# Four graph layers on one core: where one unit's division and normalization run (ScalarE or VectorE)

## The chip, the cores and the metric

The kernel runs on one core of a Trainium2 chip. The metric is the time of one execution on the device in microseconds; several executions give a median. The engines are named as the profile names them: PE is TensorE (PEld its weight loads), DVE is VectorE, ACT is ScalarE, POOL is GpSimd, SP is the queue that issues most of the DMAs.

## What is computed

The input x has 8 batches of 2048 nodes with 64 features; adj is a 2048 x 2048 matrix of edges that all batches share. Four layers follow each other, and each adds its result to x and normalizes every row over its 64 features. Cut to what matters here:

```python
# layers 0, 1, 2: attention over the edges, for each batch
s1, s2 = h @ a1, h @ a2                       # h is x times a weight matrix
e = leaky_relu(s1[:, :, None] + s2[:, None, :], 0.2)
att = softmax(where(adj > 0, e, -large), axis=-1)
h_prime = att @ h                             # then elu (layers 0, 1) or relu (layer 2)
x = layernorm(x + activation(h_prime))
# layer 3: softplus features, a softmax per feature over the edges
feat = softplus(x * c + b0)
attn = softmax(where(adj, feat * wa + ba, -large), axis=2)
x = layernorm(x + einsum(attn, feat))
```

The code counts layers from 0: "layer 1" in the code is the second layer, "layer 2" the third.

## The kernel before, in words

**Units and tiles.** A unit is one layer of one batch, written (layer, batch). The list `todo` (line 1243) orders the 24 units of the attention layers: (0,0) to (0,3), (1,0) to (1,3), (0,4) to (0,7), (1,4) to (1,7), then (2,0) to (2,7). A unit has 16 tiles, one for each block of 128 source nodes, and `attend` (line 902) computes one: a 128 x 2048 tile w of attention weights, and four matmuls that multiply it with the features and add to two PSUM tiles `acc`. In layers 0 and 1 VectorE makes w in one operation. In layer 2 a tile takes three engines in turn: GpSimd clamps a row (`clamp`, line 884, two tiles ahead), ScalarE takes two exponentials of 1024 columns into PSUM (`exponential`, line 893; two PSUM buffers), VectorE multiplies each with the edges. Four w buffers are there, so a clamp must wait until TensorE is through with the tile four places earlier.

**The order of the work.** Every engine takes its instructions in the order in which the program issues them (`InOrder`, line 68). The main loop issues the tiles; between two tiles it calls `bg.step()` once, which moves every generator in a list of background streams (`Streams`, line 1209) one step ahead. A generator that yields 2 sits out a step. So the number of yields in a stream decides between which tiles its later parts land. Streams that need a PSUM buffer of the pool `pm` (two buffers) wait their turn in `pm_slots`; `Banks.width()` says whether a stream may take both at once.

**The end of a unit** is such a stream: `finish` (line 949), begun right after the unit's last tile, so that it runs among the tiles of the unit behind it. ScalarE copies the sums to `oT`; TensorE multiplies them with a matrix (`p_o`, four products in PSUM, the 65th column of each half being the divisor); the division follows (lines 988 to 1006): a reciprocal `den` on VectorE, then, for layers 0 and 1, 16 ScalarE operations of 128 x 64, each with its own scale, and for layer 2 four VectorE operations of 128 x 256. Then the activation and the sum with x; `stats` (line 486) makes the row sums and `inv_std` the factor rs (a power on GpSimd) and the shift nm. The normalization follows (lines 1033 to 1045): 16 ScalarE operations of 128 x 64 with a yield after every fourth for layers 0 and 1, or two VectorE operations of 128 x 1024 for layer 2. A result that layer 1 or 2 goes on with is stored one column to the right, with a column of ones ahead of the features (`Rows`, line 158); its 64th feature lies in a column of its own for each block, and `settle` copies it there on GpSimd and writes the ones.

**Behind the end of (1,7)** the same stream goes on with `scores(2, 7)` (transposes `p_xT`, copies `xTv`, products `p_s`, the copy `s`), and then with `group(1)` (line 758), which makes the bounds of the clamps for the units (2,4) to (2,7): small VectorE operations on `lc`, `lim`, `sc`, `s2`, `tt`, `hi`, `lo`; 256 small matmuls `p_lse` in 8 pieces of 32, one piece in each step, and then `am`, `amT` and a DMA to the rows that unit (2,4) reads.

**Layer 3** is made of streams too: `l3_features` of a batch follows its unit of layer 2 (softplus `sp` and `f` on ScalarE with two loads of the function table, `vf`, and splitting into three bf16 parts `v`), and `l3_products` multiplies edges with a pair of batches once both are ready. `now` holds the layer of the unit whose tiles are being issued, and that unit's place in `todo`; after the last unit, now[0] is 3.

All of these operations are recorded through one helper, so the profile gives line 78 for all of them: groups are told apart by the names of their tiles. In these names layer and batch are left out, so `x<-o,st_x` stands for the normalization of every unit.

Of the kernel before, what the change touches and what calls it, by code (L numbers as in the profile page):

```python
# [14 lines left out]
ALU = mybir.AluOpType  # L15
# [33 lines left out]
def gnn4_kernel(ctx: ExitStack, tc: tile.TileContext, t, out):  # L49
# [3 lines left out]
    K = N // P  # L53
# [51 lines left out]
    class Banks:  # L105
# [4 lines left out]
        pool = None  # L110
# [28 lines left out]
    pe, dve, act, pool = (InOrder(e) for e in (nc.tensor, nc.vector, nc.scalar, nc.gpsimd))  # L139

    def psum(name):
        return pm.tile([P, 512], F32, tag="pm", name=name)

    def bc_f(v, n=K, f=F):
        return v[:, :, None].to_broadcast([P, n, f])

    def bc_k(v, n=K, f=F):
        return v[:, None, :].to_broadcast([P, n, f])
# [337 lines left out]
    def stats(y, n, name):  # L486

        st = small.tile([P, 2, n], F32, tag="st", name=f"st_{name}", bufs=4)
        yield from sq_slots.take()
        sq = tmp.tile([P, n, F], F32, tag="sq", name=f"sq_{name}")  # L490
        act.activation(sq, y, AF.Square)
        dve.tensor_reduce(st[:, 0], y, AX.X, ALU.add)
        yield 2 if now[0] < 2 else 1
        dve.tensor_reduce(st[:, 1], sq, AX.X, ALU.add)
        sq_slots.give()
        yield from inv_std(st, n, name)
        return st[:, 0], st[:, 1]
# [451 lines left out]
    def finish(u):  # L949
        layer, b = u.layer, u.b  # L950
        yield from oT_slots.take()
        oT = tmp.tile([P, 2, 512], F32, tag="oT", name=f"oT_{u.n}")
        for c in range(2):
            act.copy(oT[:, c], u.acc[c])
        if layer == 0:
            hb = early.tile([P, K, F], F32, tag="hb", name=f"hb_{u.n}", bufs=1)
            for sl, y in V[0, b].parts:
                pool.tensor_tensor(
                    hb[:, :, sl], y, bc_k(gamma[:, sl], K, y.shape[2]), ALU.mult
                )  # L960
        yield 1
        yield from o_slots.take()
        o = tmp.tile([P, K, F], F32, tag="o", name=f"o_{u.n}", bufs=2)
        o5 = o.rearrange("p (c h s) f -> p c s h f", c=2, h=2)
        done = 0
        while done < 4:
            width = Banks.width()
            ps = []
            yield from pm_slots.take(width)
            for i in range(done, min(done + width, 4)):  # L970
                c, s0 = i // 2, 2 * (i % 2)
                p = psum(f"p_o_{u.n}_{c}_{s0}")
                for s in range(2):
                    k = s0 + s
                    pe.matmul(
                        p[:, s * 2 * F1 : (s + 1) * 2 * F1],
                        lhsT=oT[:, c, k * P : (k + 1) * P],
                        rhs=RH[layer].rearrange("p h f -> p (h f)"),
                        start=True,
                        stop=True,  # L980
                    )
                ps.append((c, s0, p))
            done += width
            if done >= 4:
                oT_slots.give()
            yield 2 if width == 2 else 1
            for c, s0, p in ps:
                p4 = p[:, : 4 * F1].rearrange("p (s h f) -> p s h f", s=2, h=2)
                den = small.tile([P, 2, 2], F32, tag="den", name=f"den_{u.n}_{c}_{s0}")
                dve.reciprocal(den, p4[:, :, :, F])  # L990
                if layer == 2:
                    dve.tensor_tensor(
                        o5[:, c, s0 : s0 + 2],
                        p4[:, :, :, :F],
                        den[:, :, :, None].to_broadcast([P, 2, 2, F]),
                        ALU.mult,
                    )
                    continue
                for s in range(2):
                    for h in range(2):  # L1000
                        act.activation(
                            o5[:, c, s0 + s, h],
                            p4[:, s, h, :F],
                            AF.Copy,
                            scale=den[:, s, h : h + 1],
                        )
            pm_slots.give(width)
        if layer == 2:
            for sl, x in x_cur[b].parts:
                dve.scalar_tensor_tensor(o[:, :, sl], o[:, :, sl], 0.0, x, ALU.max, ALU.add)  # L1010
            yield 1
        else:
            yield 1
            if layer == 0:
                pool.tensor_tensor(o, o, hb, ALU.add)
                yield 2

            yield from e_slots.take()
            e = tmp.tile([P, K, F], F32, tag="e", name=f"eh_{u.n}")
            act.activation(e, o, AF.Relu, scale=-1.0)  # L1020
            act.activation(e, e, AF.Exp, scale=-1.0)
            yield 1
            for sl, x in x_cur[b].parts:
                pool.tensor_tensor(
                    e[:, :, sl], e[:, :, sl], x, ALU.add
                )
            act.activation(o, o, AF.Relu)
            yield 1
            pool.tensor_tensor(o, o, e, ALU.add)
            e_slots.give()  # L1030
            yield 2
        nm, rs = yield from stats(o, K, f"x_{u.n}")
        xn = Rows(x_cur[b].t, layer < 2)
        if layer == 2:
            dve.tensor_tensor(o, o, bc_f(rs), ALU.mult)
            dve.tensor_tensor(xn.v, o, bc_f(nm), ALU.add)
        else:
            yield 1
            for k in range(K):
                act.activation(  # L1040
                    xn.block(k), o[:, k], AF.Identity, scale=rs[:, k : k + 1], bias=nm[:, k : k + 1]
                )
                if k % 4 == 3:
                    yield 1
            xn.settle()
        o_slots.give()
        x_cur[b] = xn
        V[layer + 1, b] = xn
        if layer < 2:
            yield 1  # L1050
# [7 lines left out]
    now = [0, 0]  # L1058
# [227 lines left out]
    for n, (layer, b) in enumerate(todo):  # L1286
# [31 lines left out]
        for jb in range(K):  # L1318
            if n == 0:
                while masks < min(K, 9 + jb):  # L1320
                    mask(p_deg, masks)
                    masks += 1
                    if masks == K:
                        empties(p_deg)
            attend(u, jb, handover)
            if jb == K - 1:
                end = [lambda u=u: finish(u)]
                if layer < 2:
                    end += [2 if now[0] < 2 else 1, lambda layer=layer, b=b: scores(layer + 1, b)]
                else:  # L1330
                    end += [1, lambda b=b: l3_features(b)]
                if layer == 1 and b % NB == NB - 1:
                    end += [lambda b=b: group(b // NB)]
                bg.add(chain(*end), begun=True)
            elif not done and jb >= 10 and ready(*nxt):
                prepare(*nxt)
                done = True
            if done and nxt is not None and nxt[0] == 2 and jb >= K - 2:
                clamp(*nxt, jb - (K - 2))
            if layer == 0 and jb == 2 and 6 <= b + 4 < B:  # L1340
                load_x(b + 4)
            if n == 0 and jb == 3:
                bg.add(constants())
            if jb == (1 if n < 2 else 4) and n in begin:
                bg.add(features0(begin[n]))
            bg.step()
# [517 lines left out]
```

## Time and profile before

| | us |
|---|---|
| median of 4 runs | 1572.63 (1569.91 to 1576.92) |
| the profiled execution | 1577.95 |
| its span, first to last instruction | 1576.1 |
| PE busy in the span | 1325.7 (84%) |
| DVE busy | 1298.0 (82%) |
| POOL busy | 811.2 (51%) |
| ACT busy | 801.1 (51%) |
| mean granted TensorE clock | 0.944 |

VectorE's products of layer 2 begin at 778.85 us; the units (2,0) and (2,1) take the stretch up to 907 us. The busy shares are means over stages with different limits, so a number for one stage is read from the timeline of that stage. Times in a timeline are microseconds from the start of the span, then the length, engine, operation, tiles and shapes. A bracket at the end gives the idle time of the engine ahead of this instruction, and what ended it. An instruction's length holds the time in which it waits for the memory access it needs, so equal instructions of different length tell of such waits.

### The profile page before, as it was taken

The page shows a single profiled execution, that of the slowest core. Times are in us where ns is not written, and L with a number is a line of the kernel's source. Part 1 is how long each engine was busy: PE and PEld are TensorE (multiplying, and loading weights), DVE is VectorE, ACT ScalarE, POOL GpSimd, SP SyncE. Part 2 cuts the span into 40 slices and gives each one's busy share as a digit, 9 for nine tenths or more (in the row PEclk, how much of TensorE's full clock was granted, in tenths as well). Part 3 has the DMA queues.
Part 4 walks back from the last instruction along what each step waited for, and adds up shares of the span by engine and source line. Part 5 has one row for each costly group of instructions (what it writes and reads, how often), then busy time and mean ns, then how long its engine had stood idle before and what let it go on. Part 6 is the DMA issues. An engine that isn't in the chain of part 4 may idle for free.

```text
span 1576.1 us, 20954 instructions
## 1 busy us (share of the span) xinstructions
PE 1325.7 (84%) x8130; PEld 658.6 (42%) x8130; DVE 1298.0 (82%) x1364; ACT 801.1 (51%) x1635; POOL 811.2 (51%) x742
## 2 busy tenths in 40 slices
PE   3668888988899899998878585899977989789996
PEld 2313333333333333433222131456543646477885
DVE  4798989988999999999878878978887888777444
ACT  4315454546465434344488657575756575552110
POOL 1153353344233434232476577577879687864332
PEclk9989999999999999999999789899988999889998
DMA  8720000000000000000000000000101000000000
GB/s 307 223 42 2 1 2 1 1 2 2 1 1 2 0 1 2 1 29 28 0 1 27 27 2 27 1 27 8 35 7 34 1 7 7 8 8 15 14 13 18
DMA packets 42190, 36.86 MB, mean 23 GB/s; under 512 B 37509, under 2 KB 37813, under 8 KB 39906
## 3 DMA queue, kind: packets, MB, share of 16 engines
q1 hardware_dynamic: 41538, 34.26, 7.0%
q8 instruction: 66, 1.08, 0.3%
q10 hardware_dynamic: 544, 1.17, 0.2%
q14 instruction: 42, 0.34, 0.1%
HBM read 30.94 MB, written 4.45 MB: 22 GB/s over the span
## 4 chain that ended last, share of the span: by engine, by line
PE 24%; DVE 20%; ACT 9%; issue 5%; POOL 5%; POOLq 0%; DVEq 0%; ACTq 0%
PE p_l L78 16%; DVE w L78 11%; PE acc L78 6%; ACT e L78 4%; DVE o L78 2%; DVE st_x L78 2%; ACT sp L78 1%; POOL w L78 1%; POOL vf L78 1%; DVE vf L78 1%; ACT x L78 1%; ACT v L78 1%; DVE fs L78 1%; POOL e L78 1%; PE p_o L78 1%
## 5 line engine op out<-in xcount | busy, mean ns | idle before, releaser
L78 DVE SCALAR_TENSOR_TENSOR w<-r,se,edge 128x2048 f32<-128x2048 f32 (+1 forms) x270 | 555.4, 2102 | 22.6 <-PE r L78 19.7
L78 PE MATMUL acc<-w,pv 128*64 128x512 f32 x2048 | 504.6, 624 | 74.2 <-DVE w L78 69.0
L78 PEld LDWEIGHTS <-edge 128*128 128x128 fp8e4 x3842 | 322.5, 99 | 126.8 <-issue 65.4
L78 ACT ACTIVATE e<-w,s_g 128x1024 f32<-128x1024 f32 x256 | 277.7, 1113 | 172.0 <-DVE w L78 127.7
L78 PE MATMUL acc<-w,x 128*64 128x512 f32 x1024 | 284.8, 673 | 89.1 <-DVE w L78 84.0
L78 PE MATMUL p_l<-v,edge 128*128 128x256 bf16 x3072 | 354.1, 276 | 0.6 <-ACT nd L78 0.6
L78 DVE TENSOR_TENSOR w<-e,edge 128x1024 f32<-128x1024 f32 x256 | 299.8, 1212 | 50.5 <-ACT e L78 48.7
L78 POOL TENSOR_SCALAR w<-row,hi_g,lo_g 128x2048 f32<-128x2048 f32 x128 | 275.1, 2154 | 42.9 <-PE acc L78 39.9
L78 PEld LDWEIGHTS acc<-w,pv 128*64 128x64 f32 x2048 | 132.2, 140 | 340.8 <-issue 183.3
L78 PEld LDWEIGHTS acc<-w,x 128*64 128x64 f32 x1024 | 64.5, 147 | 239.1 <-DVE w L78 170.6
L78 ACT ACTIVATE nd<-p_l,empty 128x256 f32<-128x256 f32 x64 | 29.9, 469 | 133.2 <-PE p_l L78 133.2
L78 ACT ACTIVATE x<-o,st_x 128x64 f32<-128x64 f32 x256 | 90.3, 443 | 4.2 <-DVE st_x L78 4.2
L78 ACT COPY oT<-acc 128x512 f32<-128x512 f32 x48 | 25.7, 586 | 126.8 <-PE acc L78 126.8
L78 ACT ACTIVATE o<-p_o,den 128x64 f32<-128x64 f32 x256 | 55.8, 325 | 49.9 <-DVE den L78 49.8
L78 POOL TENSOR_TENSOR st_h<-isw_h,mhalf 128x16 f32<-128x16 f32 x8 | 23.6, 2951 | 110.3 <-DVE isw_h L78 85.4
L78 PE MATMUL p_o<-rh,oT 128*128 128x130 f32 x384 | 60.4, 295 | 20.4 <-DVE st L78 13.2
L78 POOL TENSOR_TENSOR st_x<-isw_x,mhalf 128x16 f32<-128x16 f32 x24 | 71.1, 2962 | 2.0
L78 PEld LDWEIGHTS p_o<-rh,oT 128*128 128x128 f32 x384 | 49.6, 197 | 52.2 <-issue 32.9
L78 DVE TENSOR_REDUCE st<-sq 128x4 f32<-128x256 f32 x32 | 13.2, 414 | 65.3 <-ACT sq L78 65.3
L78 POOL TENSOR_SCALAR isw_x<-isw_x 128x16 f32<-128x16 f32 x24 | 6.3, 262 | 113.7 <-DVE isw_x L78 113.7
L78 POOL CAST rT<-rT 16x128 bf16<-16x128 f32 x45 | 15.0, 333 | 95.0 <-ACT rT L78 91.9
L78 POOL TENSOR_SCALAR isw<-isw 128x4 f32<-128x4 f32 x32 | 7.4, 231 | 104.3 <-DVE isw L78 99.7
(236 smaller groups left out, 1516.9 us busy)
## 6 DMA issues: line engine op xcount, KB each, us to landing
raw<-in_adjT_dram SPq DMA_DIRECT2D x8, 1024.0 KB
raw<-in_adjT_dram SPq DMA_DIRECT2D x16, 512.0 KB
row<-rows_d_g SPq DMA_DIRECT2D x8, 1024.0 KB
x<-in_x_dram SPq DMA_DIRECT2D x8, 512.0 KB
out_dram<-o SPq DMA_DIRECT2D x64, 64.0 KB
row<-row_d ACTq DMA_DIRECT2D x1, 1024.0 KB
row_d<-rT SPq DMA_DIRECT2D x15, 12.0 KB
row<-row_d SPq DMA_DIRECT2D x15, 12.0 KB
```

The lines of the kernel that those rows point to most:

```text
L78: ins = f(*args, **kwargs)
```

## The change

The condition that chooses VectorE for the division and the normalization is no longer the unit's own layer, but the layer whose tiles are being issued at that moment. Units of layer 2 always end at a time when that is 2 or 3, so nothing changes for them. Of the other 16 units, only (1,7) comes to these lines among tiles of layer 2. For it, the division is made by four VectorE products of 128 x 256, and the normalization by a product of 128 x 1024 and a sum in two parts, of 1008 columns and of 16, which write the shifted layout at once; GpSimd writes the ones. The five yields between the ScalarE operations aren't there in that branch.

```diff
@@ in finish
                 dve.reciprocal(den, p4[:, :, :, F])
-                if layer == 2:
+                if now[0] > 1:
                     dve.tensor_tensor(
                         o5[:, c, s0 : s0 + 2],
                         p4[:, :, :, :F],
@@ in finish
         nm, rs = yield from stats(o, K, f"x_{u.n}")
         xn = Rows(x_cur[b].t, layer < 2)
-        if layer == 2:
+        if now[0] > 1:
             dve.tensor_tensor(o, o, bc_f(rs), ALU.mult)
-            dve.tensor_tensor(xn.v, o, bc_f(nm), ALU.add)
+            for sl, y in xn.parts:
+                dve.tensor_tensor(y, o[:, :, sl], bc_f(nm, K, y.shape[2]), ALU.add)
+            if layer < 2:
+                pool.memset(xn.v[:, :, 0:1], 1.0)
         else:
             yield 1
             for k in range(K):
```

## Prediction

> **What bounds the kernel now.** Read first the page's costliest groups for the third layer: each tile takes two exponentials on ScalarE and two products on VectorE, and each waits for the other.
>
> ```profile
> L78 ACT ACTIVATE e<-w,s_g 128x1024 f32<-128x1024 f32 x256 | 277.7, 1113 | 172.0 <-DVE w L78 127.7
> ...
> L78 DVE TENSOR_TENSOR w<-e,edge 128x1024 f32<-128x1024 f32 x256 | 299.8, 1212 | 50.5 <-ACT e L78 48.7
> ```
>
> Two products need 2.4 us, two exponentials 2.2 us, and there are only two PSUM buffers between them. A tile left alone lasts 2.45 us (two exponentials start at 847.52, the next two at 849.99). Whatever stands between them on either engine is then paid, unless the other engine fills the same gap. Next, VectorE's timeline: unit (1,7) ends among the tiles of unit (2,0).
>
> ```profile
> 795.31 2.35 DVE L78 TENSOR_TENSOR w<-e,edge 128x1024 f32<-128x1024 f32 x2 [2.79 <-ACT e L78]
> ...
> 801.52 2.36 DVE L78 TENSOR_TENSOR w<-e,edge 128x1024 f32<-128x1024 f32 x2 [1.39 <-ACT e L78]
> ...
> 825.62 2.36 DVE L78 TENSOR_TENSOR w<-e,edge 128x1024 f32<-128x1024 f32 x2 [1.16 <-ACT e L78]
> ...
> 868.27 0.34 DVE L78 TENSOR_REDUCE lc_g<-s 128x4 f32<-128x64 f32 x2 [3.00 <-ACT s L78]
> ...
> 914.53 2.35 DVE L78 TENSOR_TENSOR w<-e,edge 128x1024 f32<-128x1024 f32 x2 [7.67 <-ACT e L78]
> ...
> 944.81 0.78 DVE L78 SCALAR_TENSOR_TENSOR st_x<-st_x 128x16 f32<-128x16 f32 x1
> 945.52 1.21 DVE L78 TENSOR_TENSOR o<-o,st_x 128x1024 f32<-128x1024 f32 x1
> 946.76 2.96 DVE L78 TENSOR_TENSOR x<-o,st_x 128x1024 f32<-128x1024 f32 x1
> ```
>
> In brackets stands how long VectorE had nothing to do. ScalarE's timeline names the cause of the first two, and of the 7.67 us:
>
> ```profile
> 792.57 1.71 ACT L78 ACTIVATE o<-p_o,den 128x64 f32<-128x64 f32 x8
> ...
> 798.75 1.73 ACT L78 ACTIVATE o<-p_o,den 128x64 f32<-128x64 f32 x8
> ...
> 829.07 1.42 ACT L78 ACTIVATE x<-o,st_x 128x64 f32<-128x64 f32 x4
> ...
> 910.46 1.07 ACT L78 COPY oT<-acc 128x512 f32<-128x512 f32 x2 [4.92 <-PE acc L78]
> ```
>
> The copy of unit (2,1)'s sums waits for TensorE, which the table of windows (its columns: length, then busy time and count of PE, PEld, DVE, ACT, POOL, then the granted clock) shows fully busy at half clock, and then at full:
>
> ```profile
> 900.00:910.00 10.00, 10.00 (x88) 3.43 (x84) 6.75 (x7) 4.68 (x5) 4.88 (x2) 0.50 0.00 0
> 910.00:920.00 10.00, 8.77 (x130) 4.83 (x130) 5.41 (x8) 9.23 (x10) 6.59 (x3) 1.00 0.01 2
> ```
>
> **The order of instructions** of both programs differs from tile 2 of unit (2,0) to tile 8 of unit (2,2) only; SP's queue is the same, DMA for DMA. One unit, (1,7), changes: 32 ScalarE operations and one GpSimd copy go, seven VectorE operations come. And because its end yields five times fewer, all that follows it moves up: the scores of (2,7), the bounds of the second group, the 8 pieces of 32 small matmuls (p_lse). The end of unit (2,0) and the features of its fourth layer move back, since they share PSUM buffers.
>
> **Part 1, the division.** In place of 8 operations, VectorE gets two products of 0.42 us that add 0.35 each to its queue (845.12 to 845.67 is a reciprocal with its product, 0.55; the reciprocal alone steps 0.2). First pair: VectorE stands idle 0.89 us before the product at 790.17, which hides them. ScalarE's exponentials start at 792.57 instead of 794.15: -1.6. Second pair: the distance of the next products falls from 3.74 to 2.45, that of the ones before grows from 2.47 to 3.36: -0.4. Sum **-2.0 us**. The second pair of matmuls p_o, which waited 3.27 us for ScalarE to free PSUM, comes earlier as well; nobody waits for it.
>
> **Part 2, the normalization on VectorE.** The trace has its twin: at 944.81 in unit (2,1) the same shift, product and sum stand beside GpSimd's clamps and end at 949.72, 4.9 us in all. The last column (16 elements, about 0.15) comes on top; 0.78 of it is there already, and 1.16 us of idle time before the product at 825.62 cover a part: 4.9 + 0.15 - 0.78 - 1.16 = **+3.1 us**. Queued behind it are the products of tile 13, and ScalarE and TensorE behind those; no other cover is left, as ScalarE has no long work there. Bounds: the fastest rows (1.21 + 1.30 + 0.16 - 1.16) give +1.5; the slowest of each form (1.76 for o, 2.96 for x, 3.37 for o<-o,x) give 8.1 - 1.2 = +6.9. I take the twin: five of the eight such sums took 2.96, three 1.30 to 1.36. GpSimd's clamps, five in a row from 822.39, lose some 2.4 us; they are two tiles ahead.
>
> The Trainium skill (SBUF — State Buffer, "Who interferes with whom") speaks against this part: a VectorE instruction with two SBUF inputs and a GpSimd instruction that reads SBUF exclude each other for a whole instruction. Were all three to wait for a clamp of 2.04 us each, this part would come to some +6; the rows show the first product at 1.21 or 1.22 in seven of eight cases, so one wait.
>
> **Part 3, the normalization off ScalarE.** Four insertions of 1.42 us go. A lone one costs 1.0 (exponentials at 826.94 and 830.40 are 3.46 apart, against 2.47). Tile 15: 3.03 becomes 2.45, -0.6. The next two distances, 3.55 + 4.37, fall to 6.1: the copy of the sums still waits for TensorE, 4.0 us after tile 15's product starts. That is -1.8. The fourth gives way to the move of two copies xTv (1.14 together) to that very place: -0.2. Sum **-2.6 us**. GpSimd loses a copy of 0.21 and gets its memset early: nothing, it had been idle 4.64 us.
>
> **Part 4, the new order in unit (2,1),** from its product at 839.44 to the 7.67 us. VectorE does the same instructions in another order, so I compare its stalls. Before: 1.05 (an x insertion, up to 842.85), 3.00 (lc_g), 3.2 (st_x 1.64 and x 2.96, beyond 0.17 and 1.21), 3.35 (tt_g 1.99 and 1.55 beyond 0.25 and 0.22, and an idle 0.28), 1.98 (idle before 881.01, softplus on ScalarE), 0.59 (f), 7.67: 20.8 us. After:
> - xTv: 0.7. It keeps PSUM from p_o for 2 us; TensorE catches up within two tiles.
> - lc_g, now behind tile 4: it waits for ScalarE's copy s behind two exponentials, 3.8 us after a product of 2.3 starts: 1.5.
> - st_x and x: 3.2 again.
> - the s_g block: te stands behind two exponentials (0.9); GpSimd has few free buffers there (1.0): 1.9.
> - softplus lies beside that block: 0. But f has only one product ahead of it, and ScalarE needs 1.28 + 1.06 + 1.22 first: 2.4.
> - the clamp for unit (2,2)'s first tile stands behind two GpSimd products of 2.36 that wait for f: 1.2.
> - the copy oT: from the start P of tile 14's product TensorE needs, at half clock, 1.3 + 3.68 + 1.01 + 0.69 + 3.68 + 0.44 = 10.8, then 1.07 for the copy and 1.04 for the exponential that now stands next, P + 12.9; VectorE is through at P + 8.3: 4.6. At full clock (1.94, 0.96, 0.35, 1.94, 0.41) the same sum is 0.8.
>
> Together 15.5: **-5.3 us**, or -9.1 at full clock. I take half clock, since 890 to 910 show it on the same operations, with gaps like those to come.
>
> The skill (TensorE: Matmul & The Clock Gate, "What's actually happening") says that a busy window of about 3.4 us gives full clock. By that, oT would not be late and the whole sum would be -8.5; here TensorE was busy for 10 us and stayed at 0.50, so the measurement decides.
>
> **Part 5, unit (2,2).** The block am_g now stands ahead of the end of unit (2,1), where GpSimd goes from clamps to v<-vf of 4.08 us. Before, it waited 1.1 (1.34) and 1.75 (1.99). If its second product meets the long one: +2.1. Lower bound -0.2 (no change but tile spacing), upper +6.6: three products and o<-o,x behind 2.04 + 4.08 + 2.04 + 2.04 = 10.2 against 3.6. I take **+2.1**: the long operation stands next in the queue.
>
> **Sum:** -2.0 + 3.1 - 2.6 - 5.3 + 2.1 = -4.7 us. The profiled execution took 1577.95 (its span 1576.1 and 1.85 around it) and would take 1573.2. The runs shown have a median of 1572.63, 5.3 below it; I set the same gain against that: **1567.9 us**. Behind unit (2,2) the order is unchanged and every engine is late or early together, so I expect the gain to last.
>
> **Rivals.**
> 1. Full clock: the new gaps let TensorE reach 1.00 before tile 14. 1572.6 - 8.5 = 1564.1. For it: 878 to 880, where it recovered within 4 us of busy time. Against: 890 to 910.
> 2. The stall only moves: TensorE's eight p_lse pieces are the same work, and what lc_g and oT save comes back at f and at the clamps, with part 5 at nothing. Parts 1 to 3 alone give -1.5: 1571.1. For it: 2.4 and 1.2 us above are new waits.
> 3. Slower: VectorE and GpSimd wait for each other at every place. Part 2 at +6.9, part 5 at +6.6, and 2.0 more for vf behind a clamp: -2.0 - 2.6 - 5.3 + 6.9 + 6.6 + 2.0 = +5.6, 1578.2. It decides once those waits exceed parts 1, 3 and 4, 9.9 us together. For it: 2.96 in five rows of eight. Against: GpSimd is often out of buffers (39.9 us idle behind acc).
> 4. More units than one change: the order of instructions excludes it.
>
> **Chances.** Forecast 0.38, full clock 0.19, moved stall 0.27, slower 0.16. The forecast lies at the edge of 0.3% (4.7 us, about what a measurement can tell), so half of its chance is below: faster 0.42, same 0.42, slower 0.16. Leaving out the slower case's upper part and the best bounds (part 2 at +1.5 with full clock and part 5 at -0.2, -12.4): 1561 to 1576.
>
> **What would show it.** Right: exponentials two by two without gap at tiles 4 to 6 of unit (2,0); x<-o,st_x of unit (1,7) near 3 us; lc_g's idle near 1.5; the stall before unit (2,2)'s second tile near 4.6 at a clock of 0.50. Wrong: that stall at 7 or more, or am_g's products at 4 us each. From tile 9 of unit (2,2) on, both traces should run at a constant distance; a drift there would break the sum.

## The result, and the profile after

| | median, us | runs |
|---|---|---|
| before | 1573.02 (1567.8 to 1578.55) | 55 |
| after | 1576.62 (1572.43 to 1581.13) | 34 |
| ratio | 1.0023 [1.0015, 1.003] | |
| forecast | 1567.9 (1561 to 1576) | |

The change makes the kernel slower by 0.23%, 3.6 us: the other sign than the forecast's -4.7, and 0.6 us above its range. The profiled execution of after took 1575.12, its span 1573.3. Against the profiled execution of before (1577.95) that would be a gain of 2.8. That two profiles and some 90 runs disagree in sign is part of what has to be explained.

The page of after, its costliest groups of the third layer (busy time, mean ns of one, idle time before them):

```profile
L78 ACT ACTIVATE e<-w,s_g 128x1024 f32<-128x1024 f32 x256 | 277.9, 1114 | 183.7 <-DVE w L78 144.2
...
L78 DVE TENSOR_TENSOR w<-e,edge 128x1024 f32<-128x1024 f32 x256 | 299.7, 1212 | 32.7 <-ACT e L78 30.6
```

VectorE's idle time ahead of its products fell from 50.5 us to 32.7. ScalarE's, ahead of its exponentials, rose from 172.0 to 183.7. So VectorE waits 17.8 us less ahead of its products, yet the span is only 2.8 shorter: VectorE's busy time grew, from 1298.0 us to 1311.2. VectorE's timeline of after, from the normalization of (1,7) on, shows where:

```profile
821.82 1.21 DVE L78 TENSOR_TENSOR o<-o,st_x 128x1024 f32<-128x1024 f32 x1
823.07 3.03 DVE L78 TENSOR_TENSOR x<-o,st_x 128x1008 f32<-128x1008 f32 x2
...
851.11 0.34 DVE L78 TENSOR_REDUCE lc_g<-s 128x4 f32<-128x64 f32 x2 [1.30 <-ACT s L78]
...
871.12 0.57 DVE L78 TENSOR_TENSOR sc_g<-lim_g 128x4 f32<-128x4 f32 x1
...
872.11 1.61 DVE L78 TENSOR_TENSOR beyond<-beyond,far_g 128x1 f32<-128x1 f32 x1
...
873.93 3.85 DVE L78 TENSOR_SCALAR sc_g<-sc_g 128x4 f32<-128x4 f32 x2
...
879.23 1.23 DVE L78 TENSOR_TENSOR x<-o,st_x 128x1024 f32<-128x1024 f32 x1
```

The normalization took what part 2 said (near 3), and lc_g's idle time is near 1.5. The tiny sc_g block, which the prediction did not list at all, is not cheap: its two multiplications of four columns took 3.85 us. In before they took:

```profile
884.41 0.34 DVE L78 TENSOR_SCALAR sc_g<-sc_g 128x4 f32<-128x4 f32 x2
```

What stands beside them in after is on GpSimd's timeline:

```profile
869.64 8.12 POOL L78 TENSOR_SCALAR w<-row,hi_g,lo_g 128x2048 f32<-128x2048 f32 x4
...
916.95 4.06 POOL L78 TENSOR_SCALAR w<-row,hi_g,lo_g 128x2048 f32<-128x2048 f32 x2
920.98 4.05 POOL L78 TENSOR_TENSOR v<-vf,v 128x2048 bf16<-128x2048 f32 x1
925.02 4.13 POOL L78 TENSOR_SCALAR w<-row,hi_g,lo_g 128x2048 f32<-128x2048 f32 x2
```

Four clamps of 2.04 in a row end at 871.68, 873.71, 875.73 and 877.76. Of VectorE's small operations the first sum of sc_g ends at 871.69, `beyond` at 873.72, and the two multiplications at 875.76 and 877.78: each ends with a clamp. Ten operations that had needed 1.67 us from first to last need 7.05. The same in unit (2,2), VectorE in after and then in before:

```profile
919.22 1.87 DVE L78 TENSOR_TENSOR am_g<-am_g,half_ldeg 128x64 f32<-128x64 f32 x1
921.12 3.99 DVE L78 TENSOR_TENSOR am_g<-am_g,sc_g 128x64 f32<-128x64 f32 x1
925.14 1.96 DVE L78 TENSOR_SCALAR am_g<-am_g 128x64 f32<-128x64 f32 x1
927.02 0.21 DVE L78 SCALAR_TENSOR_TENSOR tt_g<-s,sc_g 128x64 f32<-128x64 f32 x1
927.26 1.96 DVE L78 TENSOR_TENSOR am_g<-am_g,tt_g 128x64 f32<-128x64 f32 x1
```

```profile
931.37 1.34 DVE L78 TENSOR_TENSOR am_g<-am_g,half_ldeg 128x64 f32<-128x64 f32 x1
932.74 1.99 DVE L78 TENSOR_TENSOR am_g<-am_g,sc_g 128x64 f32<-128x64 f32 x1
934.77 0.20 DVE L78 TENSOR_SCALAR am_g<-am_g 128x64 f32<-128x64 f32 x1
```

The second product waits out the long v<-vf (it ends at 925.11, GpSimd's at 925.03), as part 5 said. The multiplication and the last operation, am_g<-am_g,tt_g, then wait for one more clamp each: 10.3 us for a block that took 4.28. In before the block meets only the end of a row of clamps:

```profile
925.58 9.08 POOL L78 TENSOR_SCALAR w<-row,hi_g,lo_g 128x2048 f32<-128x2048 f32 x4
```

The last two of the four end at 932.63 and 934.66. Its two products end with them (932.71 and 934.73); the three operations behind, from 934.77 on, find GpSimd idle and take 0.20 to 0.22 each.

**The same stretch by stages.** Distances between starts of VectorE's products, in us; (0) to (2) are the units (2,0) to (2,2). The column "in place" is the experiment of that name below.

| from, to | before | after | in place | what lies there |
|---|---|---|---|---|
| (0) tile 3, tile 13 | 35.5 | 36.5 | 36.5 | division, normalization |
| (0) tile 13, (1) tile 1 | 13.8 | 12.4 | 12.4 | insertions on ScalarE before |
| (1) tile 1, (2) tile 1 | 75.1 | 69.1 | 72.2 | scores, sc_g, s_g, features, oT |
| (2) tile 1, tile 9 | 35.1 | 40.2 | 35.1 | am_g, end of (2,1) |
| sum | 159.5 | 158.1 | 156.2 | |

After repeats well (158.1, 158.2, 158.1 in three executions). Before doesn't: six profiled executions gave 159.5, 156.6, 156.9, 156.9, 159.3 and 156.6. Of the 2.8 us by which the profile of after is shorter than that of before, 1.4 lie in this stretch; 0.6 lie ahead of it (layer 2's first product starts at 778.22 instead of 778.85) and 0.8 behind it, where both programs do the same in the same order.

### The profile page after: what moved, and what is told of

It reads as the page before. It is cut to its first block, busy times and chain, and to the rows that moved or that the text cites. A ratio compares the mean times of both kernels' runs of the same rounds, so it can differ in the third digit from the quotient of the medians.

```text
span 1573.3 us, 20925 instructions
## 1 busy us (share of the span) xinstructions
PE 1322.3 (84%) x8130; PEld 656.9 (42%) x8130; DVE 1311.2 (83%) x1371; ACT 792.7 (50%) x1603; POOL 811.3 (52%) x741
## 4 chain that ended last, share of the span: by engine, by line
PE 23%; DVE 20%; ACT 8%; POOL 4%; issue 3%; POOLq 0%; ACTq 0%; DVEq 0%
PE p_l L78 16%; DVE w L78 10%; PE acc L78 6%; ACT e L78 4%; DVE o L78 2%; DVE st_x L78 1%; ACT sp L78 1%; POOL vf L78 1%; DVE vf L78 1%; POOL w L78 1%; ACT v L78 1%; ACT x L78 1%; POOL e L78 1%; DVE x L78 1%; DVE nd L78 1%
## 5 line engine op out<-in xcount | busy, mean ns | idle before, releaser
L78 ACT ACTIVATE e<-w,s_g 128x1024 f32<-128x1024 f32 x256 | 277.9, 1114 | 183.7 <-DVE w L78 144.2
L78 DVE TENSOR_TENSOR w<-e,edge 128x1024 f32<-128x1024 f32 x256 | 299.7, 1212 | 32.7 <-ACT e L78 30.6
L78 ACT ACTIVATE x<-o,st_x 128x64 f32<-128x64 f32 x240 | 84.6, 444 | 3.2 <-DVE st_x L78 3.2
L78 ACT ACTIVATE o<-p_o,den 128x64 f32<-128x64 f32 x240 | 52.3, 325 | 51.3 <-DVE den L78 51.3
```

What stands on the lines that cost most here:

```text
L78: ins = f(*args, **kwargs)
```

## Experiments

The theory formed from these lines: **the order costs, not the engine.** The VectorE operations of parts 1 to 3 give what was forecast (-1.5), and what moves up with the five yields meets GpSimd's clamps, in the blocks sc_g and am_g. First rival: the VectorE operations themselves cost more than was seen, and the order gives part 4's gain. Second rival: these waits only fill time that VectorE would have waited anyway, so their end would bring nothing. Third: the runs of before are favoured by the way the two are timed. Where an expectation gives a letter, it stands for one such theory.

### The engine without the order, and the order without the engine

"In place" is after with the yields put back, so that every instruction stands where it stood in before:

```diff
             if layer < 2:
                 pool.memset(xn.v[:, :, 0:1], 1.0)
+                yield 5
```

> The division and the normalization of unit (1,7) on VectorE as in the change, but the five yields are put back behind them, so that every other instruction of all engines stands where it stood before. Theory A (the new order is what costs: it sets the small VectorE blocks sc_g and am_g beside GpSimd's clamps, and the profiled execution of before was a long one): parts 1 to 3 of the prediction alone, 1.5 us below before. Theory B (the VectorE operations themselves cost, in their place): the whole 3.6 us above before. Theory C (both small, the rest is a difference in TensorE's clock): within 1 us of before.

Measured: 1571.74 against 1572.88 for before, ratio 0.9994 [0.9974, 1.0013]. "Order alone" is before with ScalarE's operations and after's order:

```diff
-            yield 1
+            late_unit = now[0] > 1
+            if not late_unit:
+                yield 1
...
-                if k % 4 == 3:
+                if k % 4 == 3 and not late_unit:
                     yield 1
```

> Division and normalization of unit (1,7) stay on ScalarE, in 16 operations each, but its five yields are left out, so that everything behind it is ordered as in the change (the 16 normalization operations stand in one row on ScalarE). Theory A: 3.6 + 1.5 = 5 us above before, with sc_g's block near 7 us instead of 1.7 and am_g's near 10 instead of 4. Theory B: within 1 us of before. The 16 operations in one row cost ScalarE 5.7 us at one place, as much as in four places, so this adds 1 or 2 us under either.

Measured: 1580.42, ratio 1.0053 [1.0032, 1.0074], the slowest of all kernels here. Two things are in it. ScalarE has the 16 operations in a row, and VectorE's product waits for them; and the two blocks are as long as in after, sc_g 7.07 and am_g 10.32. ScalarE, then VectorE, in order alone:

```profile
826.19 5.39 ACT L78 ACTIVATE x<-o,st_x 128x64 f32<-128x64 f32 x16
```

```profile
832.62 2.35 DVE L78 TENSOR_TENSOR w<-e,edge 128x1024 f32<-128x1024 f32 x2 [4.83 <-ACT e L78]
...
925.42 3.99 DVE L78 TENSOR_TENSOR am_g<-am_g,sc_g 128x64 f32<-128x64 f32 x1
929.44 1.96 DVE L78 TENSOR_SCALAR am_g<-am_g 128x64 f32<-128x64 f32 x1
```

The first costs 3.6 (17.4 instead of 13.8 in its stage); it is of this experiment alone and no part of after. What follows: the order makes both kernels that have it slower, and after without it isn't slower than before. The first rival falls.

> The changed kernel once more, for a second trace. Theory A: sc_g's block again 4 to 7 us against 1.7, am_g's 8 to 10 against 4.2, the stretch from tile 3 of unit (2,0) to tile 9 of unit (2,2) again near 158 us. Theory C: these blocks vary by several us between traces, with the clock. In time 3.6 us above before, by either.

After once more, on the same chip: 1576.43, ratio 1.0022 [1.0006, 1.0038], stretch 158.2. Since the intervals of in place and of this one overlap by a little (1.0013 and 1.0006), the two kernels are told apart by their stages: the table puts the whole difference behind tile 1 of (2,1), where nothing but the order differs. It is 2.0 us there (-3.1 and +5.1); the medians are 4.7 apart.

### The halves of the change alone

"Division alone" has only the first condition of the diff in before, "norm alone" only the second, with the yields put back as above:

```diff
-                if layer == 2:
+                if now[0] > 1:
                     dve.tensor_tensor(
                         o5[:, c, s0 : s0 + 2],
```

> Only the division of unit (1,7) on VectorE; normalization, yields and order as before. Part 1 of the prediction: the stretch from tile 3 to tile 13 of unit (2,0) 2.0 us shorter (35.5 before), the time 2 us below before or, by theory E, 1 us above it. If the trace shows less than 1 us there, part 1 was mis-sized.

Measured: 1572.68 against 1572.27, 0.9989 [0.9969, 1.001]. Timing can't show 2 us, the trace can: from tile 3 to tile 13 of (2,0) 33.52 instead of 35.45. That is -1.9 (part 1: -2.0).

> Only the normalization of unit (1,7) on VectorE, with its five yields behind it; division and order as before. Parts 2 and 3 of the prediction: +3.1 at tile 13 of unit (2,0), -2.6 behind it, so 0.5 us longer than before up to tile 1 of unit (2,1). The time within 1 us of before or, by theory E, some 3 us above.

Measured: 1573.34, 1.0004 [0.9986, 1.0022]. The same stage takes 38.4, +3.0 (part 2: +3.1). Against the profile of before, whose long stall this execution shares (7.62 for 7.67), the next two stages lose 1.4 and 1.0, together -2.4 (part 3: -2.6).

### Taking the waits away

If the blocks wait because operands lie in SBUF, which GpSimd's clamps read, then they must not wait with intermediate results in PSUM. The order stays. In `group`, sc and far become parts of the PSUM tile `p` that is there already (one copy into sc more at the end), and am stays in its `p` until its last operation; the PSUM buffers are given back that much later:

```diff
-        pm_slots.give()
...
-        dve.tensor_tensor(sc[:, 3], lim[:, 0], lim[:, 1], ALU.add)
+        q = p[:, 64 : 64 + 4 * NB].rearrange("p (a b) -> p a b", a=4)
+        far = p[:, 128:129]
+        dve.tensor_tensor(q[:, 3], p[:, :NB], lim[:, 1], ALU.add)
...
+        dve.tensor_copy(sc, q)
+        pm_slots.give()
...
+        pam = p[:, 64 : 64 + NB * K].rearrange("p (b k) -> p b k", b=NB)
...
-        dve.tensor_scalar(am, am, -1.0, TOP, ALU.mult, ALU.add)
+        dve.tensor_scalar(pam, pam, -1.0, TOP, ALU.mult, ALU.add)
...
-        dve.tensor_tensor(am, am, tt, ALU.min)
+        dve.tensor_tensor(am, pam, tt, ALU.min)
+        slots.give()
```

> The changed kernel, with the intermediate values of the two small VectorE blocks (sc_g and am_g, of both groups) kept in the PSUM buffer that they start from instead of SBUF, and one copy of 128 x 16 more; so these operations read at most one operand from SBUF (but for tt). The order is the same. Theory A (they wait for GpSimd's clamps at SBUF): sc_g's block falls from 7.05 us to about 2, am_g's from 10.3 to 2 to 4, the time by 6 to 11 us, to some 5 below before. Theory D (the waits only fill time in which VectorE would wait for the exponentials or for TensorE anyway): the blocks fall, the time stays within 2 us of the changed kernel.

Measured: 1570.83 against 1572.45, ratio 0.9975 [0.996, 0.9991]; that is 5.6 and 5.8 us below the two medians of after, and by the ratio below before too. For the four kernels of this section, as for division alone, the recorded ratio is 0.08 to 0.20% below the quotient of the two medians beside it (here 0.9990); why is not on record, so a distance from before of 3 us or less isn't taken as shown by these times, and the traces decide. VectorE's timeline of this kernel, with clamps beside both blocks as in after (from 872.57 to 882.76, and from 917.30 to 921.37, with v<-vf behind them):

```profile
875.27 0.38 DVE L78 TENSOR_SCALAR p_lim_g<-p_lim_g 128x4 f32<-128x4 f32 x2
...
877.85 2.96 DVE L78 TENSOR_TENSOR x<-o,st_x 128x1024 f32<-128x1024 f32 x1
...
919.54 0.23 DVE L78 TENSOR_TENSOR p_lse_g<-p_lse_g,half_ldeg 128x64 f32<-128x64 f32 x1
919.80 0.23 DVE L78 TENSOR_TENSOR p_lse_g<-p_lse_g,sc_g 128x64 f32<-128x64 f32 x1
920.07 0.23 DVE L78 TENSOR_SCALAR p_lse_g<-p_lse_g 128x64 f32<-128x64 f32 x1
920.21 1.23 DVE L78 SCALAR_TENSOR_TENSOR tt_g<-s,sc_g 128x64 f32<-128x64 f32 x1
921.48 0.23 DVE L78 TENSOR_TENSOR am_g<-p_lse_g,tt_g 128x64 f32<-128x64 f32 x1
...
922.29 4.26 DVE L78 SCALAR_TENSOR_TENSOR o<-o,x 128x1008 f32<-128x1008 f32 x2
```

The blocks fall from 7.05 to 2.2 and from 10.3 to 2.43; the one operation that still waits, tt_g at 1.23, is the one whose operands both lie in SBUF. `group` runs a second time, at 530 and 660 us in before, with no clamps near it: there the same operations of am_g take 0.20 to 0.26 in either memory, so the edit itself costs a copy of 0.17. The stretch falls from 158.1 to 150.6. The blocks are 4.9 + 7.9 = 12.8 us shorter, the stretch 7.5. The rest came back as waits of the same kind on the operations behind the blocks, which now meet the GpSimd work that the blocks had waited out: the sum x at 877.85 (2.96; 1.23 in after, where it stood just behind the last clamp of the row), the shift st_x ahead of it (0.69 for 0.17), and the sum o<-o,x at 922.29, which met v<-vf (4.26 for 1.30). That is 1.7 + 0.5 + 3.0 = 5.2, and 12.8 - 5.2 = 7.6. So the second rival (the waits only fill other waits, D in the expectations) falls: in the trace each microsecond of waiting that went is gained, within 0.1. With one half of the edit:

> The same for sc_g's block alone. Theory A: half of it, some 4 to 5.4 us below the changed kernel, so 1 us below before. Theory D: within 2 us of the changed kernel.

Only sc_g in PSUM: 1574.33 against 1572.45, 1.0004 [0.9987, 1.0021], stretch 155.6. That is 2.6 of the stretch for 4.9 of waits, of which x and st_x took back 2.2. The am_g half gives the other 4.9, of 7.9, of which o<-o,x took back 3.0.

> The kernel before with both blocks' values in PSUM. There sc_g's block takes 1.67 us, so it meets no clamp, and am_g's 4.28, of which some 2.9 is waiting. Theory A: sc_g 0.2 longer (one copy more), am_g's 2 to 3 us shorter, the time 2 to 3 us below before. Theory D: within 1 us of before.

The same edit in the order of before: 1574.59 against 1572.45, ratio 1.0000 [0.9982, 1.0019], stretch 154.2. There the blocks had waited little (am_g 4.28, now 1.89; sc_g 1.67, now 2.20). The last stage falls by the 2.4 us that am_g lost, from 35.12 to 32.75; the time doesn't show it.

> Division and normalization on VectorE, the order of before (five yields put back) and both blocks in PSUM. Theory A: the sum of the kernel in place (1.1 below before) and of the one before with PSUM (2 to 3 below): 3 to 4 us below before; the new order with PSUM should be 1 to 3 us faster still, since its other stalls are shorter. Theory D: 1 us below before, as in place alone.

In place with the edit: 1571.68, 0.9975 [0.9955, 0.9994], stretch 154.0. By the ratios after's order with the blocks in PSUM and this kernel are both below before, and can't be told from each other; the 1 to 3 us by which the new order was expected to be faster lie in the stretch (150.6), not in the time.

### Why the profile of before was no measure of before

Unchanged kernels, profiled again. First before:

> The kernel before once more, for a second trace. Theory A: the stall of VectorE in front of unit (2,2)'s second tile is clearly below 7.67 us (3 to 5), because TensorE reaches full clock before tile 14 of unit (2,1), and the stretch from tile 3 of unit (2,0) to tile 9 of unit (2,2) is near 155 us instead of 159.5. Theory B: 159 to 160 us again, stall 7 to 8.

It took 1577.53. VectorE's timeline of it, at the place of the 7.67 us:

```profile
915.81 2.36 DVE L78 TENSOR_TENSOR w<-e,edge 128x1024 f32<-128x1024 f32 x2 [3.11 <-ACT e L78]
```

Same program, same order, 4.6 us less. The windows of this execution (columns as in the prediction) show TensorE's clock:

```profile
895.00:898.40 3.40, 3.40 (x9) 0.54 (x5) 3.13 (x5) 2.32 (x4) 3.40 (x3) 0.50 0.00 0
...
901.80:905.20 3.40, 3.40 (x29) 1.00 (x26) 3.40 (x5) 3.40 (x4) 0.60 (x2) 0.52 0.61 251
905.20:910.00 4.80, 4.04 (x61) 1.91 (x58) 4.80 (x4) 2.29 (x3) 4.72 (x2) 0.99 0.00 0
```

Here full clock came after 3.4 us of busy TensorE, at 905.2. In the profile of before it stayed at 0.50 for 20.5 us, to 910.1, though TensorE was busy throughout the last ten. Copy oT waits for those matmuls, so the stall is long or short with the clock. All eleven profiled executions of kernels with this order agree: where the half clock ahead of oT lasted 20.5 us the stall was 7.59 to 7.67 (four), where it lasted 17.1, 5.84 and 5.86, and where it came in pieces of 3.4 and 6.8, 3.10 to 3.63 (five).

> The kernel before, for a third trace of the stretch from tile 3 of unit (2,0) to tile 9 of unit (2,2) (159.5 and 156.6 us so far, the changed kernel's 158.1 and 158.2). Theory A: the stall in front of unit (2,2)'s second tile depends on when TensorE gets its full clock; with the rest of the execution at 1417 us in the mean, the median of 1573 asks for a stretch near 154 us in a typical execution, so a stall near 1 us (7.66 and 3.11 so far). Theory E: the stretch lasts 156 to 160 in every execution, and the 3.6 us come from elsewhere.

> The same again, a fourth trace: theory A 153 to 156 us in most of these looks, with a stall of 0 to 3 us; theory E 156 to 160 us in all.

> The same again, a fifth trace: theory A 153 to 156 us in most of these looks, with a stall of 0 to 3 us; theory E 156 to 160 us in all.

> The changed kernel for a third trace. Theories A and E: the stretch lasts 158 us once more, since its stalls (sc_g 7.05, am_g 10.3) don't depend on TensorE's clock; if it falls below 157, the clock matters here too.

These four ran on another chip. Before took 1575.59, 1573.39 and 1577.36, with stalls of 3.63, 3.11 and 7.62; after 1575.12 with none there. The stretches of before are 156.9, 156.9 and 159.3: the 153 to 156 of theory A came in none, the 156 to 160 of theory E in all. So of six profiled executions of before (the last is that of the next run) four have the short stall and two the long one. Among the other five kernels in this order, division alone and norm alone have the long one, in place and in place with PSUM the middle one, before with PSUM the short one.

> The kernel before, timed against itself as the others were. Theory E (the five traces of before, a stretch of 157.8 us in the mean against the changed kernel's 158.1, are what its executions are like, and the timed runs of before that stand for the comparison lie some 3 us low for another reason, as all other kernels but one come out 3 to 5 us above what their stretches say): this copy is timed 2 to 4 us above the runs beside it. Theory G (the timing is right, traces of before happen to fall on long stalls): equal within 1 us.

Before timed against itself: 1572.45 against 1572.27, ratio 1.0001 [0.9983, 1.0019]; the third rival (the way of timing, E in this expectation) falls. Its profiled execution took 1577.05 with a stall of 3.1.

**What stays open.** The six profiled executions of before lie between 1573.39 and 1577.95, five of them 2.6 to 4.9 above its median of 1573.02; those of after (1575.12, 1576.19, 1575.12) lie below its median. (One more execution of before on the other chip, without a trace, took 1577.84.) In the traces the stretch of after (158.1) is 1.4 above that of the four short executions of before, and 0.5 above the mean of six; the medians say 3.6. The other 2 to 3 us aren't placed. Outside the stretch the six executions of before differ by 4.5 us among themselves (1414.6 to 1419.1), and after's three (1415.2 to 1416.1) lie within that. The profiled executions of before are also not typical of its times: four of six are above 1577, of the 55 timed ones six. That the stall which hangs on the clock is shorter still in the timed executions, whose traces aren't there, would fit, but it was not shown.

## Why the prediction was wrong, point by point

- **Parts 1 to 3: right.** -1.9, +3.0 and -2.4, against -2.0, +3.1 and -2.6. In place, the three together are -1.4 in the trace (84.1 to 82.7 up to tile 9 of (2,1)), forecast -1.5, and 0.9994 in time. Of part 3, 1.0 came one stage later than forecast: the fourth insertion gave 1.0, not 0.2, and the three before it 1.4, not 2.4. The prediction counts that fourth one twice, as -0.2 here and as "1.05" against "xTv: 0.7" in part 4.
- **Part 4, "20.8 us before": the step that failed first.** It took the 7.67 us for the kernel's own. It belongs to the executions with a late clock, two of six; the other four have 3.1 to 3.6. Their stage is 72.3 us, not 75.1, and the mean of all six is 73.2. So 1.9 to 2.8 us of the forecast gain were not there to be had. The last step of the sum, "I set the same gain against that", carried this into the median: a gain over an execution 5.3 us above the median was taken for a gain over the median.
- **Part 4, "15.5 us after": right in sum, by compensation.** The forecast makes this stage 75.1 - 0.2 - 5.3 = 69.6 us; it took 69.1. But sc_g, at nothing in the prediction, waited 5.4. In return st_x and x, forecast to wait 3.2, met no clamp, because sc_g had waited out the row; the s_g block waited 0.95 for 1.9; and oT didn't wait at half clock (0.88 on ScalarE, and 1.59 at vf, for 4.6). lc_g (1.30 for 1.5) and f (2.18 for 2.4) were right.
- **The clock: rival 1's condition came true, not its time.** Windows of after:

```profile
897.00:900.40 3.40, 3.40 (x23) 0.85 (x20) 3.08 (x3) 1.88 (x2) 3.40 (x3) 0.50 0.00 0
900.40:924.00 23.60, 19.35 (x253) 9.79 (x250) 20.20 (x21) 18.36 (x17) 20.20 (x9) 1.00 0.01 2
```

  After 3.4 us of busy TensorE the clock was at 1.00, before tile 14's matmuls; ScalarE waited 0.88 us for the sums, and the next product didn't wait for ScalarE (vf did, 1.59). The forecast chose half clock from the profile of before, where the same condition gave nothing for 10 us. The rule of the Trainium skill that the prediction set against it (TensorE: Matmul & The Clock Gate, "What's actually happening") fits this execution and the one at 905.2 above; it doesn't fit the profile of before. The same section says that the window of 3.4 us runs freely, so the moment varies with where in it the work lands. The traces here agree so far as each stretch of one granted clock lasts a multiple of 3.41 us. And they sort the misses. Cut at the clock's own steps, from 840 to 960 us, 22 pieces of 3.41 us at 0.50 in all kept traces show TensorE busy throughout and hold matmuls of p_lse. Twelve hold a whole group of 32 (1.01 us), among them before's from 899.9 and 903.3: behind none of them did the clock rise. In ten the edge cuts the group (0.18 to 0.85 us of it inside), in after's from 897.0 and that of 901.9 above too: behind each it rose. So whether before's stall is long goes with where the steps of the clock fall on the program; why a whole group keeps the clock down is open, and no experiment moved them.
- **Part 5, +2.1: its size.** This term is the largest that was mis-sized, by 3.0 us. The wait that it took, the second product behind v<-vf, is there (3.99 for 1.99). But the block grew by 6.0, near the bound of +6.6 that was given little weight, and the stage by 5.1 (35.1 to 40.2). The term counted one more long operation and no further clamps behind it. The rest of the block is 0.5 at the first product, and 1.8 and 1.7 at the multiplication and the last operation.
- **Rival 3's mechanism decided, and only one of its places was priced.** VectorE and GpSimd wait for each other in the blocks that moved: am_g, where the rival set +6.6, and sc_g, where it set nothing; not in the added operations (part 2 stayed at +3.0, not +6.9). The prediction looked for such waits only at large operations and at am_g's products.
- **Two sums beside the forecast are off.** The chances don't add up as written: full clock and half of the forecast make 0.38 for faster, the moved stall and the other half 0.46 for same, where it says 0.42 and 0.42. And the bound of +6.9 for part 2 counts 3.37 for o<-o,x, which the change doesn't touch: without it the slowest rows give 1.76 + 2.96 + 0.16 - 1.16 = +3.7, and rival 3 comes to +2.4 instead of +5.6, 1575.0. The forecast rests on neither.

With the two corrections the stages give, against the four short executions of before, +1.0 - 1.4 - 3.2 + 5.0 = +1.4: the right sign, and 2.2 below the measured 3.6. Against the mean of all six it is +0.5, and 3.1 below. This remainder is open.

The section that the prediction weighed against part 2 (SBUF — State Buffer, "Who interferes with whom") has the place that mattered as well: beside operations with two SBUF inputs it names tensor_scalar as one that can take the shared ports and so block with GpSimd, and reductions as free of it. The rows agree: 1.96 for 0.20 at 128 x 64 and 3.85 for 0.34 at 128 x 4 (two operations), while the reductions kept their lengths, as did far_g's tensor_scalar of 128 x 1 (0.15 at 871.92, beside a clamp).

## What to carry to other kernels

When a change takes yields or instructions out of a stream, list every block that moves, the tiny ones too, and look what GpSimd does at its new place: a chain of small dependent VectorE operations can pay for a GpSimd operation at one link after another (four of ten in sc_g, four of six in am_g), whatever its own size. Keeping the chain's intermediates in PSUM took these waits away at the cost of a copy; the next operations with two inputs in SBUF met the rest of the row. Before a long stall in a profile is booked as something to gain, see it in a second execution, above all where it hangs on TensorE's clock.

## What the runs showed of the hardware that was not expected

- A multiplication of 128 x 4 elements with one input in SBUF waits for a clamp to end (1.83 and 1.99, 3.85 for two; alone 0.34 for two), and one of 128 x 64 likewise (1.96, alone 0.20). Not every such operation does: hi_g and lo_g of before, 128 x 64 with one input, took 0.20 and 0.18 at 893.67 and 893.79, just after a clamp had begun.
- The number of such waits follows how many GpSimd operations still stand in the row beside the chain, not the size of the chain's operations: am_g met two clamps in before (4.28 us), three clamps and v<-vf in after (10.30).
- The granted clock of TensorE during the same instructions differs between executions: 20.5 us at 0.50 in one, pieces of 3.4 to 6.8 us in others, and the stall behind it with it (7.67 us, and 3.1 to 3.6).
